# The last two channels of a convolution, score and batch-norm kernel: column sums by matmul, another order of the work, outputs from two engines

## The chip, the core and the metric

The kernel runs on one core of one Trainium2 chip. The metric is the device time of one execution in microseconds. Before the change it is 904.93 us, the median of three runs (902.93 to 905.02). The span of a profiled execution, from its first to its last instruction, is shorter than that execution's device time by what lies around it.

## The reference

Two layers, on x of shape 4 x 64 x 256 x 256 (batch, channel, row, column), float32. The first is a two-dimensional causal convolution per channel with a kernel that is an outer product of two length-256 filters, plus a bias term. The second takes, per image, the Gram matrix of the 256 rows, weighs it elementwise, sums it along its last axis, adds that one number per row to the row, and normalises each channel over the whole batch:

```python
def _L1_conv_ref(x, weights, gamma, beta):
    inv_dim = 1.0 / jnp.sqrt(jnp.asarray(D, dtype=x.dtype))
    scores = jnp.einsum('bpsd,bptd->bpst', x, x) * inv_dim
    red = jnp.sum(scores * weights[None], axis=-1, keepdims=True)
    y = x + red
    mean = jnp.mean(y, axis=(0, 2, 3), keepdims=True)
    var = jnp.var(y, axis=(0, 2, 3), keepdims=True)
    y_hat = (y - mean) * jax.lax.rsqrt(var + BN_EPS)
    return y_hat * gamma[None, :, None, None] + beta[None, :, None, None]
```

`red` below is that row sum. Nothing can be written of a channel before its mean and variance are known over all four images.

## The kernel before

The 64 channels go through a software pipeline, one channel per turn of the loop `for c in range(C + 4)` (line 360). Instructions are issued in the order of the program text on each engine (`manual_schedule`), so the text is the queue of every engine. A channel's x, 4 images of 256 x 256, is one buffer `x0` of 128 partitions x 2 pairs x 4 blocks x 256; a "pair" v holds two images, one in each half of the partitions.

Per channel c the stages are, with the turn in which they run:

- turn c-1: `conv_z` (line 173), the row convolution on PE, 64 matmul instructions on 64 x 64 quarters of the array; `copy_z` brings it out of PSUM on ACT.
- turn c: `conv_x0` (line 194), the column convolution on PE, 64 matmuls; four DVE operations (line 213) add the bias term and write `x0`. Then `gram` (line 226) for pair 0 and pair 1: 32 matmuls each, and after each `weigh` (line 251) for its two images and `spread` (line 266). `weigh` is three DVE operations for one image: two that multiply scores by weights and sum along the row into `red0` (line 257), and one that leaves products `pr`, whose sum over the partitions is still to be taken (line 261). `spread` puts `red0` on a diagonal (`eye_sb`) and adds it to `pr`, giving `sp`, two operations for one image (line 271).
- end of turn c: `all_sum` (line 276), one GpSimd sum over the partitions for all four images, 128 x 1024 (line 279), into `rd`.
- turn c+1: `pick_red` (ACT, line 286) brings the second image's half into place, `add_red` (line 288) adds `red` to `x0` with two DVE operations over 1024 elements that also sum it up (line 293), and GpSimd sums those sums over the partitions (line 297).
- turn c+2: `minus_mean` and two `squares` on ACT (lines 301 to 306), a GpSimd sum (312), `root` on ACT (318 to 322).
- turns c+3 and c+4: `scale_shift`, five small DVE operations (326 to 334), and four `finish` (line 339), each an ACT operation over 512 elements and an output transfer of 256 KB issued by SP (line 343). Output buffers: 4.

All tiles of PSUM come from one ring of eight banks. In the text of a turn, `conv_x0(c)` stands before `conv_z(c + 1)`, and the two `gram` of c stand last. So in turn 63 the column convolution of channel 63 follows both Gram matrices of channel 62 on PE, and its four DVE operations (line 213) follow `add_red(61)`, `weigh` and `spread` of channel 62 on DVE. After it PE has nothing but `gram(63, 0)` and `gram(63, 1)`. Turns 64 to 67 hold only the remaining statistics and outputs.

Of the kernel before, what the change touches and what calls it, by code (L numbers as in the profile page):

```python
# [8 lines left out]
F32 = mybir.dt.float32  # L9
AF = mybir.ActivationFunctionType  # L10
ALU = mybir.AluOpType
RED = bass_isa.ReduceOp
# [3 lines left out]
B, C, S = 4, 64, 256  # L16
P = 128
# [4 lines left out]
H = P // 2  # L22
BN_EPS = 1e-5
# [16 lines left out]
def conv_scores_bn_kernel(  # L40
# [70 lines left out]
    with tc.tile_pool(name="fps", bufs=2, space=PSUM) as fps:  # L111
        rhs = zT_sb
        for layer in range(3):
# [15 lines left out]
            rhs = h  # L129
# [63 lines left out]

    def conv_x0(c, z):


        xt = [xts.pop((c, v)) for v in range(2)]
        toep, x0 = hs.pop(c), st8[c][0]
        for m in range(2):
            p2 = [ps.tile([P, 2, S], F32, tag="ps", name=f"p2_{c}_{m}_{v}") for v in range(2)]  # L200
            for i in range(2):
                for k in range(4):
                    for t in range(4):
                        v, u = t % 2, t // 2
                        rows = bass.ts(v, H)
                        nc.tensor.matmul(  # L206
                            p2[v][bass.ts(u, H), i, : S - H * k],
                            lhsT=z[rows, u, k, bass.ts(2 * m + i, H)],
                            rhs=toep[rows, 0, H * k : S], start=(k == 0), stop=(k == 3),
                        )  # L210
            for v in range(2):
                part = bass.ts(m, 2)
                nc.vector.scalar_tensor_tensor(  # L213
                    x0[:, v, part], xt[v][:, part], chan_sb[:, 0, c : c + 1],
                    p2[v][:, :, ::-1], ALU.mult, ALU.add,
                )
# [9 lines left out]
    def gram(c, v):  # L226


        xb = st8[c][0].rearrange("p v i (t s) -> p v i t s", s=H)
        gs = [ps.tile([P, 8, H], F32, tag="ps", name=f"g_{c}_{v}_{u}") for u in range(2)]  # L230

        for places in (
            ((0, slice(0, 3), slice(0, 5, 2)), (1, slice(1, 4), slice(2, 7, 2))),
            ((2, slice(2, 4), slice(3, 7, 3)), (3, slice(0, 4, 3), slice(0, 4, 3))),
        ):
            for i in range(4):
                for n in range(4):
                    u, h = n % 2, n // 2
                    rows = bass.ts(u, H)
                    m, t, o = places[h]  # L240
                    nc.tensor.matmul(  # L241
                        gs[u][bass.ts(h, H), o, :],
                        lhsT=xb[rows, v, i, m, :], rhs=xb[rows, v, i, t, :],
                        start=(i == 0), stop=(i == 3),
                    )
# [20 lines left out]
    def spread(c, b):  # L266

        _, red0, sp, pr, _ = st8[c]
        for n in range(2):
            part = bass.ts(n, P)  # L270
            nc.vector.scalar_tensor_tensor(  # L271
                sp[:, b, part], eye_sb, red0[:, b, n : n + 1], pr[:, b, part],
                ALU.mult, ALU.add,
            )

    def all_sum(c):

        _, _, sp, _, rd = st8[c]
        nc.gpsimd.partition_all_reduce(  # L279
            rd.rearrange("p b s -> p (b s)"), sp.rearrange("p b s -> p (b s)"), P, RED.add  # L280
        )

    def pick_red(c):

        rd = st8[c][4].rearrange("p (v u) s -> p v u s", u=2)
        nc.scalar.copy(rd[H:, :, 0, :], rd[H:, :, 1, :])  # L286

    def add_red(c):
# [8 lines left out]
        nc.gpsimd.partition_all_reduce(mom[:, 2:4], mom[:, 0:2], P, RED.add)  # L297
        return mom

    def minus_mean(mom):  # L300
        nc.scalar.activation(mom[:, 4:5], mom[:, 2:3], AF.Identity, bias=mom[:, 3:4])  # L301
        nc.scalar.activation(mom[:, 5:6], mom[:, 4:5], AF.Identity, scale=-1.0 / (B * S * S))
# [33 lines left out]
        )  # L336
        return g, sh

    def finish(c, g, sh, v, n):
        part = bass.ts(n, 2)  # L340
        o = wk.tile([P, 2, S], F32, tag="o", name=f"o_{c}_{v}_{n}", bufs=4)
        nc.scalar.activation(o, st8[c][0][:, v, part], AF.Identity, bias=sh, scale=g)  # L342
        nc.sync.dma_start(out[c, v, n], o)

    for n in range(4):
        load_h(1, n)
# [5 lines left out]
    def begin_z(c):  # L352
        zs[c] = wk.tile([P, 2, 4, S], F32, tag="z", name=f"z_{c}")
# [3 lines left out]
        copy_z(0, u, conv_z(0, u))  # L357

    moms, scales, fins = {}, {}, {}
    for c in range(C + 4):  # L360
        p, q, f, e = c - 1, c - 2, c - 3, c - 4
        if c + 1 < C:
            copy_h(c + 1)
        if c < C:
            begin(c)
            conv_x0(c, zs.pop(c))

        if c + 1 < C:
            load_w(c + 1)
        if c + 2 < C:  # L370
            load_h(c + 2, 0)
        if 0 <= q < C:
# [8 lines left out]
        if 0 <= q < C:  # L381
            squares(q, moms[q], 1)
            tot = sum_squares(q, moms[q])
        if 0 <= f < C:
            fins[f] = (f, *scale_shift(f, moms.pop(f), *scales.pop(f)))
        if c + 1 < C:
            begin_z(c + 1)
            copy_z(c + 1, 0, conv_z(c + 1, 0))
# [6 lines left out]
        if c + 1 < C:  # L395
            copy_z(c + 1, 1, conv_z(c + 1, 1))
        if 0 <= f < C:
# [7 lines left out]
        if 0 <= q < C:  # L405
            scales[q] = root(q, tot)
        if 0 <= f < C:
            finish(*fins[f], 0, 1)
        if c + 3 < C:
            load_xt(c + 3, 1, 1)  # L410
        if c < C:
            gram(c, 0)
        if 0 <= p < C:
            moms[p] = add_red(p)
        if c < C:
            gram(c, 1)
            all_sum(c)


# [66 lines left out]
```

## Time and profile before

| What | Value |
|---|---|
| median of the runs | 904.93 us |
| the profiled execution, device time | 908.73 us |
| its span | 906.9 us |
| PE busy | 854.6 us (94%) |
| DVE busy | 757.4 us (84%) |
| ACT busy | 625.4 us (69%) |
| GpSimd busy | 442.8 us (49%) |
| last matmul of the kernel ends | 877.6 us |
| last ACT operation ends | 903.8 us |

Times within a trace are counted from the start of its span. A group's "mean ns of one" is the time from an instruction's start to its end; neighbours on DVE and ACT overlap by some tens of nanoseconds, so the step from one to the next is shorter (the line-293 operation has a mean of 1219 ns, and the step between two is 1150 ns). PE's records are two for each float32 matmul instruction. "PEclk" is the granted clock of PE as a share of full speed.

### The profile page before, as it was taken

Reading aid. Unit: us, or ns where it says so; the run is one execution under the profiler, and the core shown is the slowest. Engines: PE = TensorE matmul, PEld = TensorE weight load, DVE = VectorE, ACT = ScalarE, POOL = GpSimd, SP = SyncE. Lnnn points to the kernel's source line nnn. Section 1 sums busy time; section 2 is a strip of 40 time slices with the busy share of each in tenths; the row PEclk is TensorE's granted clock in tenths of the full one; section 3 lists DMA queues with packets and bytes.
Section 4 is the critical chain, followed back from the end, with each engine's and each line's share of the span. In section 5 each row is a group of like instructions: output and inputs, shape, how many; then the busy total and the mean of one; then the engine's idle time right before and its main releaser. Section 6 shows DMA issues by size and latency. Waiting matters only on the chain.

```text
span 906.9 us, 55787 instructions
## 1 busy us (share of the span) xinstructions
PE 854.6 (94%) x24584; PEld 824.9 (91%) x24584; DVE 757.4 (84%) x2648; ACT 625.4 (69%) x1220; POOL 442.8 (49%) x196
## 2 busy tenths in 40 slices
PE   2999999999999999999999999999999999999950
PEld 1999999999999999999999999999999988999950
DVE  3369888888988998898889889888988988988892
ACT  1237677677767767776777677677767767667756
POOL 0054455455455545644554554455455445445542
PEclk9999999999999999999999999999999999999985
DMA  5443665565556656565665656666665566556424
GB/s 157 133 136 126 202 206 194 182 205 194 200 199 208 198 194 211 198 195 198 207 195 194 213 186 198 199 207 198 201 205 194 191 194 198 189 192 206 133 74 160
DMA packets 89834, 169.42 MB, mean 187 GB/s; under 512 B 10614, under 2 KB 11832, under 8 KB 89592
## 3 DMA queue, kind: packets, MB, share of 16 engines
q1 hardware_dynamic: 88572, 164.95, 54.7%
q8 instruction: 193, 3.16, 1.5%
q10 hardware_dynamic: 1020, 0.90, 0.4%
q14 instruction: 49, 0.40, 0.2%
HBM read 97.91 MB, written 67.76 MB: 183 GB/s over the span
## 4 chain that ended last, share of the span: by engine, by line
PE 93%; DVE 3%; issue 1%; ACT 1%; POOL 1%; DMA 0%; ACTq 0%; DVEq 0%
PE p L183 31%; PE p L206 31%; PE g L241 31%; DVE x L293 1%; POOL rd L279 1%; ACT o L342 1%; DVE junk L257 0%; DVE sp L271 0%; PE ph L116 0%; DVE pr L261 0%; DVE fa L125 0%; DVE x L213 0%; DMA fw_sb<-in_fw 0%; DVE fa L118 0%; ACT sq L306 0%
## 5 line engine op out<-in xcount | busy, mean ns | idle before, releaser
L279 POOL PARTITION_ALL_REDUCE rd<-sp x64 | 391.9, 6123 | 198.5 <-DVE sp L271 196.0
L183 PE MATMUL p<-toep,xt 64*64 64x256 f32 (+3 forms) x8192 | 305.4, 298 | 5.8 <-issue 5.8
L206 PE MATMUL p<-toep,z 64*64 64x256 f32 (+3 forms) x8192 | 307.6, 297 | 2.7 <-issue 2.3
L241 PE MATMUL g<-x 64*64 64x192 f32 (+1 forms) x8192 | 305.4, 297 | 2.7 <-DVE x L213 2.5
L206 PEld LDWEIGHTS p<-toep,z 64*64 64x64 f32 x8192 | 291.9, 133 | 16.0 <-issue 5.6
L183 PEld LDWEIGHTS p<-toep,xt 64*64 64x64 f32 x8192 | 288.5, 134 | 16.5 <-issue 6.8
L241 PEld LDWEIGHTS g<-x 64*64 64x64 f32 x8192 | 289.5, 134 | 6.1 <-DVE x L213 3.0
L257 DVE SCALAR_TENSOR_TENSOR junk<-g,w 128x192 f32<-128x192 f32 x512 | 161.2, 352 | 93.2 <-PE g L241 93.2
L342 ACT ACTIVATE o<-x,sh,g 128x512 f32<-128x512 f32 x256 | 207.5, 813 | 2.0 <-DVE sh L334 2.0
L213 DVE SCALAR_TENSOR_TENSOR x<-xt,chan_sb,p 128x512 f32<-128x512 f32 x256 | 174.0, 743 | 9.6 <-PE p L206 9.6
L192 ACT COPY z<-p 128x512 f32<-128x512 f32 x256 | 135.3, 580 | 36.4 <-PE p L183 35.8
L293 DVE SCALAR_TENSOR_TENSOR x<-x,rd 128x1024 f32<-128x1024 f32 x128 | 151.3, 1219 | 5.7 <-ACT rd L286 5.7
L297 POOL PARTITION_ALL_REDUCE mom<-mom x64 | 25.6, 400 | 251.8 <-DVE x L293 244.1
L306 ACT ACTIVATE sq<-x,mom 128x1024 f32<-128x1024 f32 x128 | 146.5, 1145 | 2.3
L271 DVE SCALAR_TENSOR_TENSOR sp<-eye_sb,red,pr 128x128 f32<-128x128 f32 x512 | 144.7, 345 | 0.0
L261 DVE SCALAR_TENSOR_TENSOR pr<-g,w 128x256 f32<-128x256 f32 x256 | 107.4, 420 | 0.0
L286 ACT COPY rd<-rd 64x512 f32<-64x512 f32 x64 | 39.5, 617 | 92.3 <-POOL rd L279 92.3
L301 ACT ACTIVATE mom<-mom 128x1 f32<-128x1 f32 x64 | 19.0, 297 | 94.7 <-POOL mom L297 94.7
L151 ACT COPY toep<-toep 64x512 f32<-64x512 f32 x63 | 39.0, 619 | 32.2 <-DMA toep<-g_dram 19.3
L257 DVE DVE_READ_ACCUMULATOR junk<-g,w 128x1 f32 x512 | 42.8, 83 | 0.0
L312 POOL PARTITION_ALL_REDUCE tot<-mom x64 | 30.8, 481 | 3.8 <-ACT sq L306 3.8
L306 ACT ACTIVATION_READ_ACCUMULATOR sq<-x,mom 128x1 f32 x128 | 24.0, 188 | 0.0
(33 smaller groups left out, 171.1 us busy)
## 6 DMA issues: line engine op xcount, KB each, us to landing
xt<-in_xT SPq DMA_DIRECT2D x256, 256.0 KB
out<-o SPq DMA_DIRECT2D x256, 256.0 KB
w<-in_wl SPq DMA_DIRECT2D x64, 320.0 KB
toep<-g_dram SPq DMA_DIRECT2D x252, 36.0 KB
g_dram<-g_sb ACTq DMA_DIRECT2D x4, 80.0 KB
g_dram<-g_sb SPq DMA_DIRECT2D x4, 80.0 KB
fw_sb<-in_fw ACTq DMA_DIRECT2D x1, 192.0 KB
decay_sb<-in_decay ACTq DMA_DIRECT2D x1, 128.0 KB
```

Source lines behind the costliest of these rows:

```text
L183: nc.tensor.matmul(p1[u][bass.ts(v, H), k, : S - H * i], lhsT=xts[c, v][rows, i, bass.ts(2 * m + k, H)], rhs=toep[rows, 1, H * i : S], sta ...
L192: nc.scalar.copy(zs[c][:, u, bass.ts(m, 2), :], p1[u][:, :, ::-1])
L206: nc.tensor.matmul(p2[v][bass.ts(u, H), i, : S - H * k], lhsT=z[rows, u, k, bass.ts(2 * m + i, H)], rhs=toep[rows, 0, H * k : S], start=(k ...
L213: nc.vector.scalar_tensor_tensor(x0[:, v, part], xt[v][:, part], chan_sb[:, 0, c : c + 1], p2[v][:, :, ::-1], ALU.mult, ALU.add,)
L241: nc.tensor.matmul(gs[u][bass.ts(h, H), o, :], lhsT=xb[rows, v, i, m, :], rhs=xb[rows, v, i, t, :], start=(i == 0), stop=(i == 3),)
L257: nc.vector.scalar_tensor_tensor(junk, g[:, part, :], 1.0 / math.sqrt(S), w[:, 3 * n : 3 * n + 3, :], ALU.mult, ALU.mult, accum_out=red0[: ...
L261: nc.vector.scalar_tensor_tensor(pr[:, b].rearrange("p (t s) -> p t s", s=H), g[:, COL, :], 1.0 / math.sqrt(S), w[:, 6:10, :], ALU.mult, A ...
L271: nc.vector.scalar_tensor_tensor(sp[:, b, part], eye_sb, red0[:, b, n : n + 1], pr[:, b, part], ALU.mult, ALU.add,)
L279: nc.gpsimd.partition_all_reduce(rd.rearrange("p b s -> p (b s)"), sp.rearrange("p b s -> p (b s)"), P, RED.add)
L293: nc.vector.scalar_tensor_tensor(x0[:, v], x0[:, v], 1.0, rd[:, 2 * v, None, :].to_broadcast([P, 4, S]), ALU.mult, ALU.add, accum_out=mom[ ...
L306: nc.scalar.activation(sq, st8[c][0][:, v], AF.Square, bias=mom[:, 5:6], accum_out=mom[:, 6 + v : 7 + v])
L342: nc.scalar.activation(o, st8[c][0][:, v, part], AF.Identity, bias=sh, scale=g)
```

## The change

The loop runs over channels 0 to 62 only, and everything after it is written out in a new function `last_channels(63)`. Within the loop the instructions of turns 0 to 61 are the same. In turn 62 `gram(62, 1)`, its `weigh`, all `spread` of channel 62 and `all_sum(62)` are gone from the loop. `red` of channels 62 and 63 is taken by `red_by_pe`: for each half of the partitions three matmuls into PSUM, one with a matrix of ones over `pr` (256 columns) and two with `red0`, repeated over 64 columns, over the identity (128 columns each). `add_red_of` adds it from PSUM. In `last_channels` the column convolution of channel 63 stands in front of the second half of channel 62's Gram matrix. The squares of channel 63 are taken around the mean of its first pair, and corrected by five small DVE operations afterwards. The outputs of the last three channels are shared between DVE and ACT, and there are 8 output buffers instead of 4. The constant `ones` is set once at the start.

```diff
+    ones = const.tile([P, H], F32, name="ones")
+    nc.vector.memset(ones, 1.0)
...
+    def gram(c, v, weighed=True):
...
+        if not weighed:
+            banks.extend((g,) for g in gs)
+            return
         for u in range(2):
             weigh(c, 2 * v + u, gs[u])
-        for u in range(2):
-            spread(c, 2 * v + u)
+        if c < C - 2:
+            for u in range(2):
+                spread(c, 2 * v + u)
...
+    def red_by_pe(c, v):
+        _, red0, _, pr, _ = st8[c]
+        rp = ps.tile([P, S], F32, tag="ps", name=f"rp_{c}_{v}")
+        for u in range(2):
+            b, half = 2 * v + u, bass.ts(u, H)
+            nc.tensor.matmul(rp[half], lhsT=ones, rhs=pr[:, b], start=True, stop=False)
+            for n in range(2):
+                nc.tensor.matmul(
+                    rp[half, bass.ts(n, P)], lhsT=red0[:, b, n : n + 1].to_broadcast([P, H]),
+                    rhs=eye_sb, start=False, stop=(n == 1),
+                )
+        return rp
+
+    def add_red_of(c, v, rp, mom):
+        x0 = st8[c][0]
+        nc.vector.scalar_tensor_tensor(
+            x0[:, v], x0[:, v], 1.0, rp[:, None, :].to_broadcast([P, 4, S]),
+            ALU.mult, ALU.add, accum_out=mom[:, v : v + 1],
+        )
...
+    def finish(c, g, sh, v, n, vector=False):
         part = bass.ts(n, 2)
-        o = wk.tile([P, 2, S], F32, tag="o", name=f"o_{c}_{v}_{n}", bufs=4)
+        o = wk.tile([P, 2, S], F32, tag="o", name=f"o_{c}_{v}_{n}", bufs=8)
+        if vector:
+            nc.vector.tensor_scalar(o, y, g, sh, ALU.mult, ALU.add)
...
+    def last_channels(c):
+        p, q, f, e = c - 1, c - 2, c - 3, c - 4
+        begin(c)
+        finish(*fins[e], 1, 0)
+        finish(*fins[e], 1, 1)
+        conv_x0(c, zs.pop(c))
+        minus_mean(moms[q])
+        squares(q, moms[q], 0)
+        squares(q, moms[q], 1)
+        tot = sum_squares(q, moms[q])
+        fins[f] = (f, *scale_shift(f, moms[f], *scales[f]))
+        finish(*fins[f], 0, 0)
+        mom_p = sm.tile([P, 8], F32, tag="mom", name=f"mom_{p}")
+        add_red_of(p, 0, red_by_pe(p, 0), mom_p)
+        gram(p, 1)
+        scales[q] = root(q, tot)
+        finish(*fins[f], 0, 1)
+        gram(c, 0, weighed=False)
+        add_red_of(p, 1, red_by_pe(p, 1), mom_p)
+        nc.gpsimd.partition_all_reduce(mom_p[:, 2:4], mom_p[:, 0:2], P, RED.add)
+        finish(*fins[f], 1, 0)
+        finish(*fins[f], 1, 1)
+        for u in range(2):
+            weigh(c, u, *banks.pop(0))
+        minus_mean(mom_p)
+        squares(p, mom_p, 0)
+        squares(p, mom_p, 1)
+        tot_p = sum_squares(p, mom_p)
+        gram(c, 1)
+        mom = sm.tile([P, 8], F32, tag="mom", name=f"mom_{c}")
+        add_red_of(c, 0, red_by_pe(c, 0), mom)
+        nc.gpsimd.partition_all_reduce(mom[:, 2:3], mom[:, 0:1], P, RED.add)
+        rp = red_by_pe(c, 1)
+        add_red_of(c, 1, rp, mom)
+        fins[q] = (q, *scale_shift(q, moms[q], *scales[q]))
+        half = 2.0 / (B * S * S)
+        nc.scalar.activation(mom[:, 5:6], mom[:, 2:3], AF.Identity, scale=-half)
+        squares(c, mom, 0)
+        scales[p] = root(p, tot_p)
+        squares(c, mom, 1)
...
+        nc.gpsimd.partition_all_reduce(sums[:, 1:2], mom[:, 1:2], P, RED.add)
+        nc.gpsimd.partition_all_reduce(sums[:, 2:4], mom[:, 6:8], P, RED.add)
+        for v in range(2):
+            for n in range(2):
+                finish(*fins[q], v, n, vector=n == 0)
+        fins[p] = (p, *scale_shift(p, mom_p, *scales[p]))
+        d = sums[:, 4:5]
+        nc.vector.tensor_scalar(d, sums[:, 1:2], mom[:, 2:3], half / 2, ALU.subtract, ALU.mult)
+        nc.vector.tensor_scalar(mom[:, 5:6], mom[:, 5:6], d, None, ALU.subtract)
+        nc.vector.tensor_scalar(sums[:, 5:6], d, d, -BN_EPS, ALU.mult, ALU.add)
+        nc.vector.tensor_scalar(
+            sums[:, 6:7], sums[:, 2:3], sums[:, 3:4], half / 2, ALU.add, ALU.mult
+        )
+        v = sums[:, 7:8]
+        nc.vector.tensor_scalar(v, sums[:, 6:7], sums[:, 5:6], None, ALU.subtract)
+        r = sm.tile([P, 1], F32, tag="r", name=f"r_{c}")
+        nc.scalar.activation(r, v, AF.Sqrt)
+        for i in range(2):
+            finish(*fins[p], i, 0)
+            finish(*fins[p], i, 1, vector=True)
+        fins[c] = (c, *scale_shift(c, mom, v, r))
+        for i in range(2):
+            finish(*fins[c], i, 0)
+            finish(*fins[c], i, 1, vector=True)
...
-    for c in range(C + 4):
+    for c in range(C - 1):
...
         gram(c, 0)
-        if 0 <= p < C:
+        if p >= 0:
             moms[p] = add_red(p)
-        if c < C:
+        if c < C - 2:
             gram(c, 1)
             all_sum(c)
+    last_channels(C - 1)
```

More of the change, by code (lines that the diff above doesn't have):

```diff
@@ L224, in begin @@
         st8[c] = (x0, red0, sp, pr, rd)
-    def gram(c, v):
+    banks = []
+    def gram(c, v, weighed=True):
         xb = st8[c][0].rearrange("p v i (t s) -> p v i t s", s=H)
@@ L337, in scale_shift @@
         return g, sh
-    def finish(c, g, sh, v, n):
+    def finish(c, g, sh, v, n, vector=False):
         part = bass.ts(n, 2)
-        o = wk.tile([P, 2, S], F32, tag="o", name=f"o_{c}_{v}_{n}", bufs=4)
-        nc.scalar.activation(o, st8[c][0][:, v, part], AF.Identity, bias=sh, scale=g)
-        nc.sync.dma_start(out[c, v, n], o)
+        o = wk.tile([P, 2, S], F32, tag="o", name=f"o_{c}_{v}_{n}", bufs=8)
+        y = st8[c][0][:, v, part]
+        if vector:
+            nc.vector.tensor_scalar(o, y, g, sh, ALU.mult, ALU.add)
+        else:
+            nc.scalar.activation(o, y, AF.Identity, bias=sh, scale=g)
+        nc.sync.dma_start(out[c, v, n], o)
@@ new lines, in last_channels @@
+    def last_channels(c):
[38 more added lines that the diff above has]
+        squares(c, mom, 1)
+        tot = sm.tile([P, 3], F32, tag="tot", name=f"tot_{c}")
+        sums = sm.tile([P, 8], F32, tag="sums", name=f"sums_{c}", bufs=1)
+        nc.gpsimd.partition_all_reduce(sums[:, 1:2], mom[:, 1:2], P, RED.add)
[22 more added lines that the diff above has]
+            finish(*fins[c], i, 1, vector=True)
@@ L359, in conv_scores_bn_kernel @@
     moms, scales, fins = {}, {}, {}
-    for c in range(C + 4):
+    for c in range(C - 1):
         p, q, f, e = c - 1, c - 2, c - 3, c - 4
-        if c + 1 < C:
-            copy_h(c + 1)
-        if c < C:
[L365 to L369, printed above, removed]
+        begin(c)
+        copy_h(c + 1)
+        conv_x0(c, zs.pop(c))
+        load_w(c + 1)
         if c + 2 < C:
             load_h(c + 2, 0)
-        if 0 <= q < C:
+        if q >= 0:
             minus_mean(moms[q])
@@ L380, in conv_scores_bn_kernel @@
             load_xt(c + 3, 0, 0)
-        if 0 <= q < C:
+        if q >= 0:
             squares(q, moms[q], 1)
             tot = sum_squares(q, moms[q])
-        if 0 <= f < C:
+        if f >= 0:
             fins[f] = (f, *scale_shift(f, moms.pop(f), *scales.pop(f)))
-        if c + 1 < C:
-            begin_z(c + 1)
-            copy_z(c + 1, 0, conv_z(c + 1, 0))
+        begin_z(c + 1)
+        copy_z(c + 1, 0, conv_z(c + 1, 0))
         if e >= 0:
@@ L394, in conv_scores_bn_kernel @@
             load_xt(c + 3, 1, 0)
-        if c + 1 < C:
-            copy_z(c + 1, 1, conv_z(c + 1, 1))
-        if 0 <= f < C:
+        copy_z(c + 1, 1, conv_z(c + 1, 1))
+        if f >= 0:
             finish(*fins[f], 0, 0)
@@ L402, in conv_scores_bn_kernel @@
             load_xt(c + 3, 0, 1)
-        if 0 <= p < C:
+        if p >= 0:
             pick_red(p)
-        if 0 <= q < C:
+        if q >= 0:
             scales[q] = root(q, tot)
-        if 0 <= f < C:
+        if f >= 0:
             finish(*fins[f], 0, 1)
@@ L410, in conv_scores_bn_kernel @@
             load_xt(c + 3, 1, 1)
-        if c < C:
-            gram(c, 0)
-        if 0 <= p < C:
+        gram(c, 0)
+        if p >= 0:
             moms[p] = add_red(p)
-        if c < C:
+        if c < C - 2:
             gram(c, 1)
             all_sum(c)
+    last_channels(C - 1)
 def kernel(**inputs):
```

## The prediction

> **What bounds the kernel now.** The page comes first: its span, the shares of the chain that ended last, and the slices. For 877 of 906.9 us the chain is PE's matmuls, and the change leaves PE's instructions of that stretch as they are. So the gain is to be sought in the end, where PE has stopped.
>
> ```profile
> span 906.9 us, 55787 instructions
> PE   2999999999999999999999999999999999999950
> PE 93%; DVE 3%; issue 1%; ACT 1%; POOL 1%; DMA 0%; ACTq 0%; DVEq 0%
> ```
>
> Second, the chain of waits in order of time (start, us, what). After channel 63's last `spread` DVE stops, GpSimd sums for 6.13 us, ACT copies, DVE adds: all in a row.
>
> ```profile
> 881.93 1.05 DVE sp L271 x4
> 882.98 0.08 DVE r L326
> 883.06 0.08 issue
> 883.14 6.13 POOL rd L279
> 889.28 0.02 issue
> 889.30 0.63 ACT rd L286
> 889.92 0.02 issue
> 889.95 2.38 DVE x L293 x4
> ```
>
> Third, the timeline of the end: the Gram matrices of channel 63 wait for its column convolution, and the last seven outputs come from ACT alone, one each 0.74 us.
>
> ```profile
> 869.88 2.71 DVE L213 SCALAR_TENSOR_TENSOR x<-xt,chan_sb,p 128x512 f32<-128x512 f32 x4
> 870.67 0.88 PE L241 MATMUL g<-x 64*64 64x192 f32 x16 [2.07 <-DVE x L213]
> 871.99 5.60 PE L241 MATMUL g<-x 64*64 64x192 f32 x112 [0.44 <-DVE x L213]
> 898.60 5.20 ACT L342 ACTIVATE o<-x,sh,g 128x512 f32<-128x512 f32 x7
> ```
>
> Fourth, stretches of it (us; busy PE, PE loads, DVE, ACT, GpSimd; clock, DMA share, GB/s). PE's clock falls to half after its idle time, and a burst of outputs fills the DMA engines at about 370 GB/s. No byte moves after 905.5, so 1.5 us of the span follow the last byte.
>
> ```profile
> 873.00:874.00 1.00, 1.00 (x24) 1.00 (x20) 0.74 (x4) 0.12 (x1) 1.00 (x1) 0.50 0.68 246
> 886.00:886.50 0.50, 0.00 (x0) 0.00 (x0) 0.00 (x0) 0.00 (x0) 0.50 (x1) 0.50 0.99 373
> 904.00:904.50 0.50, 0.00 (x0) 0.00 (x0) 0.00 (x0) 0.00 (x0) 0.00 (x0) 0.50 1.02 381
> 905.50:906.00 0.50, 0.00 (x0) 0.00 (x0) 0.00 (x0) 0.00 (x0) 0.00 (x0) 0.50 0.00 0
> ```
>
> **What the Trainium skill says.** "TensorE: Matmul & The Clock Gate", Part 1: PE runs at half clock after an idle window of about 3.4 us. The trace agrees in kind (0.50 after PE's gaps from 868.6 on). "VectorE: DVE Perf Modes", Mode 2×_2P: a float32 operation with a single tensor source and both sides in SBUF takes two elements per cycle; here TENSOR_SCALAR over 256 takes 294 ns (lines 122, 123) and SCALAR_TENSOR_TENSOR over 256 takes 425 ns (line 125). "DMA: Bandwidth & Descriptors", Specifications: 358 GB/s of HBM for a core, 368 in a cost model; the trace shows 373 and 381 in half microseconds. "TensorEngine Tiling (Array Packing)", Key Properties: a change of the tiling mode drains PE; `red_by_pe` (128 rows x 64 columns) among 64 x 64 tiles makes such changes, and no row of before shows their cost.
>
> **The change, part by part**, on the clock of the profiled execution.
>
> *Start and loop: nothing.* `ones` is a memset of 128 x 64 (0.11 us for such a one, line 101) while DVE has been idle up to 3.96 us. Eight output buffers take away waits of ACT on transfers that cost nothing: line 342's idle time is 2.0 us in all, behind DVE.
>
> *DVE from 863.85.* `pick_red(61)` ends at 863.83. Before, `spread` of channel 62 held DVE until 864.76; now `add_red(61)` starts at once: 2 x 1.15 = 2.29, to 866.14. Then come the four line-213 operations of channel 63, 2.71, to 868.85; their matmuls are ready, since `gram(62,0)` ends near 861.9 (half of 859.6 to 864.0), and `conv_x0(63)` takes 4.55, to 866.45. So channel 63's x is complete 3.7 us earlier than before (872.59). `scale_shift(60)`: 1.35 (872.51 to 873.84 before), to 870.2.
>
> *`red_by_pe`, unknown.* 128 records of `conv_z` with 2,560 column steps take 4.55 us, 1.78 ns per column. A half has 256+128+128 = 512 columns: 0.91 us if its loads (133 ns, two per matmul) are hidden; with all six in the open 0.91 + 0.80 = 1.7. Two halves use different columns of the array and might overlap, which gives a lower bound of 0.45 per half. I take 1.0, as loads of 133 ns exceed the 114 ns of a 128-column record, and 0.17 us from last issue to result (a 64-column record lasts 217 ns, of which 57 are columns).
>
> *PE*: `red_by_pe(62,0)` 866.45 to 868.45; `gram(62,1)` and `gram(63,0)`, 2.3 each (half of 4.6), to 873.05; `red_by_pe(62,1)` to 875.05, result 875.2; `gram(63,1)` to 877.35. PE has no gap until 877, so I keep full clock.
>
> *DVE on.* `add_red_of` reads PSUM: between 1.15 (line 293's step) and 1.36 (two line-213 steps of 0.68, 512 elements from PSUM); I take 1.25. Channel 62 pair 0 to 871.45; `weigh` of two images, 1.78 (861.93 to 863.71), to 873.23; then DVE waits 2.0 for `red_by_pe(62,1)`. Pair 1 to 876.45. `weigh` of channel 63, 4 x 0.89, to 880.0. Pair 0 of 63 to 881.25. Its last sums: image 1 is weighed at 878.23, three halves on PE follow, to 881.25 + 0.17 = 881.4; pair 1 to 882.65. Before this was 892.33. **Gain so far 9.7 us**: the GpSimd sum with its copy (883.14 to 889.92) and the 3.7 us of the order, less the new waits on PE.
>
> *Statistics.* The sum of pair 0 starts 0.16 after 881.25, takes 0.40 (line 297), ACT's mean 0.2; squares from 882.1: 1.25 (893.49 to 894.74), `root(62)` 0.7, squares 1.25, to 885.3, GpSimd to 885.8. DVE meanwhile: `scale_shift(61)` to 884.0; two outputs, estimated 294 + 133 = 0.43 each, to 884.85; `scale_shift(62)` to 886.2; five small operations of 0.26, to 887.5. So here DVE, not the squares, ends last, and squaring from the first pair's mean gains nothing by itself. Square root to 887.8, two outputs of 62 on DVE to 888.35, `scale_shift(63)` to 889.7. From complete x to known scale: 7.05 us, before 7.54 (892.33 to 899.87).
>
> *Outputs.* ACT makes two of channel 62 from 887.8 (0.74 each), two of 63 by 891.2; DVE's are ready sooner. SP issues in program order, 0.35 apart: the first of 62 at 888.6, the last of 63 at 891.6. From an issue (883.29) to its bytes is 0.75 us; 256 KB at 370 GB/s is 0.71; after the last byte 1.5. Eight outputs in a burst: 888.6 + 0.75 + 8 x 0.71 + 1.5 = 896.5. Production alone would give 891.6 + 0.75 + 0.71 + 1.5 = 894.6. **The transfers take back 1.9 us of what sharing the outputs gives.** From known scale to the end stays near 7 us (before 899.87 to 906.9).
>
> *Sum.* 906.9 - 896.5 = 10.4 us, of which 9.7 from `red` and order, 0.5 from the statistics, 0.2 from the outputs. The profiled execution would go from 908.73 to 898.3; it lies 3.8 above the median, so the gain comes off the median: 904.93 - 10.4 = 894.5 us.
>
> **The rivals.** *Outputs do not queue:* DMA engines show 0.99 to 1.02 of their time busy in such a burst, which speaks against it, but channel 62 could be out sooner. Then 894.6 ends the span: 892.6 us. *`red_by_pe` is slow, or PE cools:* loads in the open (0.7 more for each of seven halves in series: 4.9), or half clock in the waits after 875 (two to three halves and half of a Gram matrix, about 4): 898 to 899.5. For it: the mode changes and loads into the same rows; against it: PE is fed without a gap until 877. *Slower than before:* both together. Each `red_by_pe` drains PE, loads in the open and runs at half clock, 3.4 us for a half; seven in series are 7 x 2.4 = 17 us more, 911 us. It decides from 1.0 + (10.4 + 2.7)/7 = 2.9 us for a half. The trace shows half clock only after gaps of PE, and nothing that lengthens loads threefold. *The change doesn't do what it says*, a wait on a PSUM bank that holds the column convolution back: the ring of eight gives it banks freed at 860.9 and 863.7, so I see none; with it `red` alone would still be worth 6 us: 899.
>
> **How the numbers follow.** Forecast 894.5 with chance 0.55 (893 to 896.5 of its own); outputs don't queue 0.15; slow or cool PE, or the bank, 0.25; slower 0.03; what is left, 0.02, near no change. The range reaches from 891.5 (the second case with `red_by_pe` at 0.45) to 898.8. A measurement of this kernel tells 0.3% (2.7 us) from no change. Faster 0.95, same 0.02, slower 0.03.
>
> **What would show it.** No GpSimd sum of 6 us after 863.2; `add_red_of` of channel 63's second pair ending near 882.6; a half of `red_by_pe` near 1.0 us; DVE idle about 2 us before `add_red_of` of channel 62's pair 1; DVE's small operations, not the squares, ahead of the square root; the DMA engines full from 889.4 to 895. I am wrong if the loop's turns change length, if a half takes 2 us or more, or if the last bytes follow the last issue with no queue.

## The result, and the profile after

The change makes the kernel faster: 893.89 us (median of 6 runs, 890.46 to 895.64) against 905.34 us (6 runs, 902.93 to 907.40) for the kernel before on the same chip. The ratio is 0.9865, with a 95% interval of 0.9838 to 0.9892, a gain of 11.45 us (9.8 to 14.7 by that interval). The prediction had 894.5 and 10.4.

The profiled execution of after took 891.24 us, and its span of 889.2 is 17.7 shorter than that of before. Not all of this is the change's. But for one small memset and the number of output buffers, both kernels contain the same instructions up to channel 61's GpSimd sum (128 x 1024). It starts at 857.04 before and at 851.04 after, so 6.0 us of the difference arose in the loop before it. Some turns of the loop last longer than the usual 13.08 us, and each execution has its own number of them. All comparisons of traces below therefore use one number, **T: from the start of channel 61's GpSimd sum to the end of the span**. Before it is 906.9 - 857.04 = 49.86 us, after 889.2 - 851.04 = 38.16 us, so the end gained 11.7 us. "rel" below counts from that start. In the trace of before it is this line (the same line of after stands below):

```profile
857.04 6.13 POOL L279 PARTITION_ALL_REDUCE rd<-sp  x1 [2.43 <-DVE sp L271]
```

The page of after (span; busy share of PE and granted PE clock in 40 slices; shares of the chain that ended last):

```profile
span 889.2 us, 55809 instructions
PE   2999999999999999999999999999999999999993
PEclk9999999999999999999999999999999999999997
PE 96%; DVE 2%; issue 1%; ACT 0%; DMA 0%; ACTq 0%; DVEq 0%
```

GpSimd has left the chain altogether (1% before), and PE's part rose from 93% to 96%: PE is now busy into the last slice instead of leaving that one and half of the one before empty.

The chain of waits of after in order of time (start, us, what):

```profile
872.36 0.51 PE rp L314 x2
872.87 0.44 PE rp L316 x4
873.31 0.39 PE rp L314 x2
873.70 0.45 PE rp L316 x4
874.15 0.02 issue
874.17 1.23 DVE x L324 x2
...
881.72 0.28 DVE sh L363
882.01 0.03 issue
882.03 0.81 ACT o L375
882.85 0.71 ACTq L581
```

PE carries the chain until 874.15 (rel 23.1); the two halves of `red_by_pe(63,1)` are 0.51 + 0.44 = 0.95 and 0.39 + 0.45 = 0.84 us in it. Channel 63's x is complete at 875.40 (rel 24.4; before 892.33, rel 35.3). The last scale is known at 882.0.

The timeline of after (start, duration, engine, line, operation; in brackets the idle time before it and who ended it):

```profile
851.04 6.12 POOL L287 PARTITION_ALL_REDUCE rd<-sp  x1 [2.43 <-DVE sp L279]
868.21 1.22 DVE L324 SCALAR_TENSOR_TENSOR x<-x,rp 128x1024 f32<-128x1024 f32 x1 [1.17 <-PE rp L316]
876.70 1.00 DVE L373 TENSOR_SCALAR o<-x,g,sh 128x512 f32<-128x512 f32 x2
877.87 1.50 ACT L375 ACTIVATE o<-x,sh,g 128x512 f32<-128x512 f32 x2
```

851.04 is the last 128 x 1024 sum of the kernel; those of channels 62 and 63 are gone. DVE's wait for PE (the second line) is 1.17 us. Two outputs take DVE 1.00 and ACT 1.50. Note the third and fourth line: DVE has two outputs of channel 61 ready by 877.7, but ACT makes its first only from 877.87, since `squares` of channel 63 stands in front.

Stretches of after (from:to and length, us; busy PE, PE loads, DVE, ACT, GpSimd; PE clock, DMA share, GB/s):

```profile
872.00:874.00 2.00, 2.00 (x16) 1.47 (x14) 2.00 (x7) 1.12 (x2) 0.40 (x1) 1.00 0.00 0
879.00:879.50 0.50, 0.00 (x0) 0.00 (x0) 0.39 (x4) 0.37 (x1) 0.00 (x0) 0.83 0.00 0
879.50:880.00 0.50, 0.00 (x0) 0.00 (x0) 0.47 (x4) 0.07 (x1) 0.00 (x0) 0.50 0.94 348
885.00:886.00 1.00, 0.00 (x0) 0.00 (x0) 0.00 (x0) 0.00 (x0) 0.00 (x0) 0.50 1.02 377
887.00:887.50 0.50, 0.00 (x0) 0.00 (x0) 0.00 (x0) 0.00 (x0) 0.00 (x0) 0.50 0.42 156
887.50:888.00 0.50, 0.00 (x0) 0.00 (x0) 0.00 (x0) 0.00 (x0) 0.00 (x0) 0.50 0.00 0
```

PE runs at full clock while it still has work; its clock drops around 879, when it has none. The last burst of transfers starts at 879.5, fills the DMA engines, and ends at about 887.2. In these 7.7 us eleven outputs of 256 KB go out, 0.70 us each. Some 2.0 us of the span follow the last byte.

### The profile page after: what moved, and what is told of

Same layout as the page of the kernel before. It is cut to its first block, busy times and chain, and to the rows that moved or that the text cites. A ratio compares the mean times of both kernels' runs of the same rounds, so it can differ in the third digit from the quotient of the medians.

```text
span 889.2 us, 55809 instructions
## 1 busy us (share of the span) xinstructions
PE 855.8 (96%) x24632; PEld 818.4 (92%) x24632; DVE 757.5 (85%) x2644; ACT 615.8 (69%) x1209; POOL 430.9 (48%) x195
## 4 chain that ended last, share of the span: by engine, by line
PE 96%; DVE 2%; issue 1%; ACT 0%; DMA 0%; ACTq 0%; DVEq 0%
PE p L185 32%; PE p L208 32%; PE g L245 31%; PE ph L118 0%; PE rp L314 0%; PE rp L316 0%; DVE fa L127 0%; DMA fw_sb<-in_fw 0%; DVE fa L120 0%; DVE o L373 0%; ACT fh L130 0%; PE ph_out L133 0%; DVE x L324 0%; DVE fk L125 0%; DVE fa L128 0%
## 5 line engine op out<-in xcount | busy, mean ns | idle before, releaser
L287 POOL PARTITION_ALL_REDUCE rd<-sp x62 | 379.6, 6122 | 193.8 <-DVE sp L279 193.8
L185 PE MATMUL p<-toep,xt 64*64 64x64 f32 (+3 forms) x8192 | 304.3, 298 | 5.8 <-issue 5.8
L208 PE MATMUL p<-toep,z 64*64 64x64 f32 (+3 forms) x8192 | 303.4, 297 | 0.7 <-issue 0.5
L185 PEld LDWEIGHTS p<-toep,xt 64*64 64x64 f32 x8192 | 283.9, 134 | 20.8 <-issue 6.8
L245 PE MATMUL g<-x 64*64 64x192 f32 (+1 forms) x8192 | 300.9, 296 | 0.0
L208 PEld LDWEIGHTS p<-toep,z 64*64 64x64 f32 x8192 | 285.2, 134 | 16.7 <-issue 1.3
L245 PEld LDWEIGHTS g<-x 64*64 64x64 f32 x8192 | 286.4, 134 | 2.3 <-issue 0.3
L375 ACT ACTIVATE o<-x,sh,g 128x512 f32<-128x512 f32 x250 | 201.6, 809 | 0.7 <-DVE sh L363 0.7
L301 DVE SCALAR_TENSOR_TENSOR x<-x,rd 128x1024 f32<-128x1024 f32 x124 | 146.6, 1219 | 0.1
L279 DVE SCALAR_TENSOR_TENSOR sp<-eye_sb,red,pr 128x128 f32<-128x128 f32 x496 | 140.2, 344 | 0.0
L294 ACT COPY rd<-rd 64x512 f32<-64x512 f32 x62 | 38.2, 616 | 93.0 <-POOL rd L287 92.9
L335 ACT ACTIVATION_READ_ACCUMULATOR sq<-x,mom 128x1 f32 x128 | 23.9, 186 | 0.0
```

The source lines that it names most:

```text
L185: nc.tensor.matmul(p1[u][bass.ts(v, H), k, : S - H * i], lhsT=xts[c, v][rows, i, bass.ts(2 * m + k, H)], rhs=toep[rows, 1, H * i : S], sta ...
L208: nc.tensor.matmul(p2[v][bass.ts(u, H), i, : S - H * k], lhsT=z[rows, u, k, bass.ts(2 * m + i, H)], rhs=toep[rows, 0, H * k : S], start=(k ...
L245: nc.tensor.matmul(gs[u][bass.ts(h, H), o, :], lhsT=xb[rows, v, i, m, :], rhs=xb[rows, v, i, t, :], start=(i == 0), stop=(i == 3),)
L279: nc.vector.scalar_tensor_tensor(sp[:, b, part], eye_sb, red0[:, b, n : n + 1], pr[:, b, part], ALU.mult, ALU.add,)
L287: nc.gpsimd.partition_all_reduce(rd.rearrange("p b s -> p (b s)"), sp.rearrange("p b s -> p (b s)"), P, RED.add)
L301: nc.vector.scalar_tensor_tensor(x0[:, v], x0[:, v], 1.0, rd[:, 2 * v, None, :].to_broadcast([P, 4, S]), ALU.mult, ALU.add, accum_out=mom[ ...
```

## The experiments

T below comes from the trace of one execution of each kernel. Where a device time is given too, it is a median of several runs, and its ratio is to the kernel before on the same chip. The controls come first, because a single trace is only worth something if T repeats.

| Run | What differs | T, us | against after (38.14) |
|---|---|---|---|
| c_before | the kernel before | 50.05 | +11.9 |
| c_after, c2_after | after, on two chips | 38.14, 38.12 | 0 |
| e1_act_outs | all outputs on ACT | 39.02 | +0.9 |
| e2_full_mean | squares from the mean of both pairs | 39.16 | +1.0 |
| e6_old_order | column convolution behind Gram | 37.97 | -0.2 |
| e9_sum_alone | e1, e2 and e6 together: the sum by PE is what is left | 40.37 | +2.2 |
| e5_pool_sum | sums back on GpSimd | 53.26 | +15.1 |
| e3_half_bytes | half the bytes of the last outputs | 36.52 | -1.6 |
| e7_bufs8 | before, with 8 output buffers | 48.89 | +10.8 |
| e4_early61 | channel 61's outputs earlier | 37.25 | -0.9 |
| e8_early_both | those of 61 and 62 earlier | 35.45 | -2.7 |

**Controls.**

> The kernel before once more, as a control of T. Theory 1 (T of before depends only on whether PE's clock drops to half in channel 63's Gram matrices): T is 49.9 us with clock 0.5 there, as in the first trace, or 48.9 with clock 1.00, as with eight output buffers. Theory 2: T lies elsewhere by 0.7 us or more, and the gain of T is not known to better than that.

> The changed kernel once more, as a control. T is the time from the start of channel 61's GpSimd sum (128 x 1024) to the end of the span: 49.9 us in the trace of before (906.9 - 857.0), 38.2 in that of after (889.2 - 851.0). Theory 1: what differs between executions of one kernel lies in the loop's turns, so T comes out within 0.5 us of 38.2 whatever the span is. Theory 2: the end varies too, then T lies 1 us or more away and single traces of the experiments can't be compared by T.

> The changed kernel on the same chip as the one before, for comparison with it. Both theories: T 38.2 within 0.3; ratio to before 0.984 to 0.990.

T is 49.86 and 50.05 for before, 38.16, 38.14 and 38.12 for after. In after, c_after, c2_after, e1 and e2, whose work on PE and DVE is the same up to there, channel 63's x is complete at rel 24.35 each time. The start of channel 61's sum meanwhile lies at 851.04, 863.56 and 855.68 in the three executions of after, and on one single chip at 863.56 to 869.53 in seven executions of after and its variants. So one trace tells differences in T above some 0.2 us, and the span doesn't tell 5 us. Six runs of c2_after had a median of 897.02 (895.46 to 901.74), ratio 0.9866 (0.9823 to 0.9910), the first result again.

**e1_act_outs: are the shared outputs worth something?**

```diff
-        if vector:
+        if False:
```

> All twelve outputs of channels 61 to 63 by ACT, none by DVE. Theory 1 (the outputs are bound by their transfers, 0.69 us each, in either kernel): ACT makes one in 0.74 us, so it is only a little slower than the transfers: the last output is issued near 2.7 us later than in after, with no queue behind it, and T rises by 0.5 to 1.2 us, to 38.7 to 39.4. Theory 2 (two engines at the outputs are a main part of the gain): six outputs back on ACT are 4.4 us more in its queue, T rises by 3 us or more, to 41 or above.

T grew by 0.9, within the 0.5 to 1.2 of the first theory. Two stretches of e1 and, below them, two of after:

```profile
896.00:896.50 0.50, 0.00 (x0) 0.00 (x0) 0.00 (x0) 0.50 (x2) 0.00 (x0) 0.50 0.08 29
904.00:905.00 1.00, 0.00 (x0) 0.00 (x0) 0.00 (x0) 0.00 (x0) 0.00 (x0) 0.50 1.00 373
```

```profile
878.00:878.50 0.50, 0.00 (x0) 0.00 (x0) 0.43 (x3) 0.50 (x1) 0.41 (x1) 1.00 0.76 287
878.50:879.00 0.50, 0.00 (x0) 0.00 (x0) 0.46 (x3) 0.50 (x2) 0.00 (x0) 1.00 0.64 238
```

In e1 the burst begins at 896.45 (rel 28.5, as in after) and is full until 905.0: 8.6 us, the time of twelve outputs. In after, 287 and 238 GB/s over half a microsecond each are 262 KB: one output, the first that DVE made, is gone before the burst begins, and eleven remain. ACT alone makes one output in 0.72 us (eight in 5.73), about the 0.70 in which the queue takes one, so the faster making in the middle of the burst brings little: what sharing gives is that one output ahead of it.

**e2_full_mean: is squaring from the first pair's mean worth something?**

```diff
-        nc.gpsimd.partition_all_reduce(mom[:, 2:3], mom[:, 0:1], P, RED.add)
...
+        nc.gpsimd.partition_all_reduce(mom[:, 2:4], mom[:, 0:2], P, RED.add)
...
-        squares(c, mom, 0)
         scales[p] = root(p, tot_p)
+        minus_mean(mom)
+        squares(c, mom, 0)
         squares(c, mom, 1)
...
+        tot = sum_squares(c, mom)
...
+        v, r = root(c, tot)
```

> The squares of channel 63 wait for the mean of both pairs, without the five correcting operations on DVE; channel 62's root moves in front of them. Theory 1 (DVE's small operations and the transfers end last, not the squares): T within 0.7 us of 38.2, since the squares start 1.7 us later but 0.9 us of corrections go and the transfers are full either way. Theory 2 (squaring from the first pair's mean is worth its 1.15 us plus the wait for the second sum): T rises by 1.5 us or more.

T grew by 1.0. Its timeline and two stretches of it:

```profile
890.40 1.00 DVE L373 TENSOR_SCALAR o<-x,g,sh 128x512 f32<-128x512 f32 x2
...
891.54 1.15 ACT L335 ACTIVATE sq<-x,mom 128x1024 f32<-128x1024 f32 x1
...
892.68 1.50 ACT L375 ACTIVATE o<-x,sh,g 128x512 f32<-128x512 f32 x2
```

```profile
893.00:894.00 1.00, 0.00 (x0) 0.00 (x0) 0.70 (x2) 1.00 (x2) 0.74 (x1) 0.50 0.00 0
894.00:895.00 1.00, 0.00 (x0) 0.00 (x0) 0.16 (x1) 0.97 (x5) 0.00 (x0) 0.50 0.67 250
```

T fits neither theory; it lies between them. The scale of channel 63 is known only 0.4 later than in after (from T's start: 31.3 against 31.0). But the later `squares` also hold back the outputs of channel 61 that ACT makes: the first starts at 892.68 (rel 27.9; after 877.87, rel 26.8). SP issues in program order, so the outputs that DVE has ready wait behind it, and the burst begins at about 894.35 (rel 29.6; after rel 28.5). A queue that is full from end to end passes on its start: 1.1 later at its head, 1.0 at its end.

**e6_old_order: is the new order worth something?** `gram(p, 1)` goes back in front of the column convolution.

```diff
+        gram(p, 1)
         conv_x0(c, zs.pop(c))
...
-        gram(p, 1)
```

> The column convolution of channel 63 stands again behind the whole Gram matrix of channel 62; the sums by PE, statistics and outputs are those of after. Theory 1 (DVE bounds this stretch, its work is the same in either order, and the 1.17 us it waits for PE take up the rest): T within 0.5 us of 38.2. Theory 2 (the order itself is worth the 2 to 3.7 us that the prediction gave to it): T 40 to 42.

T fell by 0.2: beside the sum by PE, the new order is worth nothing. Three pieces of its chain of waits:

```profile
876.50 4.58 PE p L208 x92
...
891.94 0.45 PE rp L316 x4
...
892.42 1.23 DVE x L324 x2
```

Here too PE works through to `red_by_pe` of the last pair, and x is complete at 893.65, rel 24.1 (after 24.4), so the new order rather costs 0.2 us. In either order PE then holds the chain from the convolution to the last sums, with the same work (the two pairs of `red_by_pe(62)` take 1.50 us each here, 1.50 and 1.87 in after). What the order would be worth without the sum by PE was not measured.

**e9_sum_alone: e1, e2 and e6 in one kernel.** What is left of the change is the sum by PE (and what goes with it: no `spread`, no GpSimd sum, no copy, for two channels), the 8 buffers, and the text of `last_channels`, which makes the outputs of channel 61 later than before does.

> Only the sum over the partitions of channels 62 and 63 by PE: the column convolution in the old order, the squares from the full mean, all twelve outputs of channels 61 to 63 by ACT. Theory 1 (the sum by PE, with spread and the copy gone, is nearly the whole gain; the rest is worth 0.9 and 1.0 us as measured singly): T 39.5 to 40.5. Theory 2 (the parts need one another, as the slow run with GpSimd in the new order might suggest): T 43 or above.

T is 40.37, 9.5 below before and within the first theory's range. Its chain shows how the gain comes and how part of it goes back:

```profile
882.03 1.23 DVE x L324 x2
...
886.94 2.82 ACT o L375 x4
```

x of channel 63 is complete at 883.26, rel 23.9, which is 11.4 earlier than before (35.3). But from there to the end it takes 16.4 us instead of 14.6 before. In e9 ACT makes all four outputs of channel 61 (886.94) between complete x and the last scale, and all eight of channels 62 and 63 after them. In before it makes three outputs in that place (894.64 and 896.49):

```profile
890.66 0.80 ACT L342 ACTIVATE o<-x,sh,g 128x512 f32<-128x512 f32 x1
...
894.64 0.80 ACT L342 ACTIVATE o<-x,sh,g 128x512 f32<-128x512 f32 x1
...
896.49 1.51 ACT L342 ACTIVATE o<-x,sh,g 128x512 f32<-128x512 f32 x2
```

Of the four outputs in these lines the first, at 890.66, comes before x is complete (892.33); it is channel 61's second, and its first was made beside the GpSimd sum. The shared outputs and the first pair's mean win these 1.9 us back, and more: after needs 13.8 us from complete x to the end. Taken out singly they cost 0.9 and 1.0, together with the order 2.2, so about 0.5 comes only where both are there.

**e5_pool_sum: the other way round, everything but the sum by PE.**

```diff
-        add_red_of(p, 0, red_by_pe(p, 0), mom_p)
         gram(p, 1)
+        all_sum(p)
...
-        gram(c, 0, weighed=False)
-        add_red_of(p, 1, red_by_pe(p, 1), mom_p)
+        gram(c, 0)
+        gram(c, 1)
+        all_sum(c)
...
+        pick_red(p)
+        add_red_by_pool(p, mom_p)
```

> The sum over the partitions of channels 62 and 63 goes back to GpSimd (with spread on DVE and the copy on ACT), in the new order of the convolution, with the new statistics and the shared outputs. T as before, from the start of channel 61's GpSimd sum to the end. Theory 1 (taking the sum from GpSimd and spread from DVE is nearly the whole gain of 11.7 us): the two sums of 6.13 us run back to back, channel 63's x is complete about 8 us later than in after, T 45.5 to 47. Theory 2 (the order and the outputs carry the gain): T 40 to 42.

53.26 fits neither theory: it is longer than the T of before. The timeline says why:

```profile
884.01 6.12 POOL L286 PARTITION_ALL_REDUCE rd<-sp  x1 [2.71 <-DVE sp L278]
885.54 3.94 DVE L278 SCALAR_TENSOR_TENSOR sp<-eye_sb,red,pr 128x128 f32<-128x128 f32 x4
...
892.48 6.95 POOL L286 PARTITION_ALL_REDUCE rd<-sp  x1 [2.34 <-DVE sp L278]
893.37 5.55 DVE L310 SCALAR_TENSOR_TENSOR x<-x,rd 128x1024 f32<-128x1024 f32 x1
```

Four `spread` operations, 1.12 us when GpSimd is idle, took 3.94 beside its sum; the second `add_red` operation of channel 62 took 5.55, and the sum beside it 6.95 instead of 6.12. Both kinds read two tensors from SBUF. The 2.8 and 4.3 us are together about what T lies above the 45.5 to 47 of the first theory. The first `add_red` operation (at 892.23) took its usual 1.21, though the sum began 0.25 us after it and ran beside the rest, so not every part of a sum slows such an operation. The `weigh` operations beside the first of these sums, with one operand in PSUM, kept their 0.34 to 0.36 for `junk` and 0.42 for `pr`. The Trainium skill states it in "GPSIMD Engine Reference", 1. Specifications: GpSimd's SBUF interfaces are shared with VectorE, with contention for DVE instructions that have two SBUF inputs; "SBUF — State Buffer", Who interferes with whom, says it of a GpSimd instruction that reads SBUF. This run agrees and gives the price. In before neither kind runs beside such a sum (in one turn, `spread` ends at 842.78, the sum lasts from 842.95 to 849.07, the next `spread` starts at 850.63). So e5 measures the collision together with the sum, and doesn't give the sum's own worth. For that there is e9.

**e7_bufs8: do the 8 buffers do something by themselves?** The kernel before, with `bufs=8` for the outputs.

```diff
-        o = wk.tile([P, 2, S], F32, tag="o", name=f"o_{c}_{v}_{n}", bufs=4)
+        o = wk.tile([P, 2, S], F32, tag="o", name=f"o_{c}_{v}_{n}", bufs=8)
```

> The kernel before with eight output buffers instead of four, nothing else changed. Theory 1 (the buffers do nothing; the 6 us by which the loop was shorter in the one trace of after is scatter between executions): the ratio to before lies within 0.4% of 1, and T within 0.3 us of 49.9. Theory 2 (fewer waits of ACT on transfers shorten the loop): the ratio is 0.996 or lower.

The device time is 915.33 us (20 runs), ratio 1.0009 (0.9986 to 1.0031), no difference. Yet its T is 48.89, 1.0 to 1.2 below the two traces of before and outside the first theory's 0.3. A stretch within `gram(63)`, first of c_before, then of e7:

```profile
880.00:881.00 1.00, 1.00 (x20) 0.85 (x16) 0.81 (x4) 0.00 (x0) 1.00 (x1) 0.50 0.76 262
```

```profile
879.00:880.00 1.00, 1.00 (x36) 0.96 (x36) 0.86 (x4) 0.00 (x0) 1.00 (x1) 1.00 0.31 98
```

c_before did 20 matmul records there in a microsecond at clock 0.50, e7 36 at 1.00. Its x of channel 63 is complete at rel 34.5 instead of 35.3 in the trace of before: 0.8 of the difference is in this stretch, the rest, 0.15, behind the last scale. So in both executions of before PE was at half clock there, and in the one of e7 it was not. PE's idle time just before `gram(63)` doesn't tell them apart: 2.07 and 2.08 us where the clock fell, 2.14 where it didn't, all shorter than the 3.4 us of idle time that the prediction gives as the condition. Whether the buffers have to do with it, or the chip (e7 and c_before were on different ones), stays open. Against a before with full clock the sum by PE alone gives 48.9 - 40.4 = 8.5.

**e3_half_bytes: do the last transfers queue?** The last twelve outputs are written by half only.

```diff
+        if c < C - 3:
+            nc.sync.dma_start(out[c, v, n], o)
+        else:
+            nc.sync.dma_start(out[c, v, n][:, 0:1], o[:, 0:1])
```

> The transfers of the last three channels carry the first half of each output buffer only; all computation stays. Theory 1 (the end waits for a queue of transfers that began with channel 61): the last transfer follows its issue without a queue, the end comes 1.5 to 2.5 us sooner, T 35.7 to 36.7. Theory 2 (the end is bound by making and issuing the outputs): T within 0.4 us of 38.2.

T fell by 1.6, as the first theory had it. Two stretches of it:

```profile
898.00:899.00 1.00, 0.00 (x0) 0.00 (x0) 0.00 (x0) 0.00 (x0) 0.00 (x0) 0.50 0.80 266
899.00:900.00 1.00, 0.00 (x0) 0.00 (x0) 0.00 (x0) 0.00 (x0) 0.00 (x0) 0.50 0.04 12
```

With half the bytes the engines move 266 GB/s at a share of 0.80, no longer full, and 128 KB take 0.49 us. So the bytes of the last outputs account for 1.6 us of T, the shorter transfer of the very last one included. What sets the 0.49 was not separated.

**e4_early61 and e8_early_both: can the burst begin earlier?** e4 takes `scale_shift(61)` and its outputs in front of channel 63's statistics. e8 does this for channel 62's as well, except for one output of each, and swaps the engines that make channel 63's:

```diff
+        rp_p = red_by_pe(p, 1)
+        fins[q] = (q, *scale_shift(q, moms[q], *scales[q]))
+        add_red_of(p, 1, rp_p, mom_p)
...
+        finish(*fins[q], 0, 0)
+        finish(*fins[q], 0, 1)
...
+        finish(*fins[q], 1, 0)
+        scales[p] = root(p, tot_p)
...
+        fins[p] = (p, *scale_shift(p, mom_p, *scales[p]))
...
+        finish(*fins[p], 0, 0, vector=True)
+        finish(*fins[q], 1, 1, vector=True)
+        finish(*fins[p], 1, 0)
+        finish(*fins[p], 1, 1)
...
+        finish(*fins[p], 0, 1, vector=True)
```

> Channel 61's scale is worked out while DVE waits for the second sum by PE of channel 62, and its four outputs are made by ACT in its idle time around 868 to 870 and 873 to 875, so that eight instead of twelve outputs stand in the last burst and DVE has 2.3 us less between channel 63's x and its scale. Theory 1 (the burst of transfers that begins with channel 61 sets the end): it begins with channel 62 instead, and the last output lands 2 to 3 us sooner: T 35.2 to 36.2, median about 891.5 against about 894 of after. Theory 2 (the statistics of channel 63 set the end, transfers don't queue): only DVE's 0.9 us come off, T about 37.3.

> Beyond the early channel 61: channel 62's root goes in front of the squares of channel 63, its scale follows channel 63's x at once, and its outputs start before the five correcting operations, so that the burst of transfers begins about 2 us sooner than with channel 61 early alone (T 37.3). Theory 1 (the time from the first output of the last eight to the end is that of eight transfers plus 2.7 us): T 35 to 36, median 2 to 3 us below that of after on the same chip. Theory 2 (the scale of channel 63 now ends last): T about 36.5.

T is 37.25 for e4 (-0.9) and 35.45 for e8 (-2.7). e4 has the T of its second theory but not its reason: the transfers do queue. Its burst begins with channel 62, as in the first theory, but at 897.25 (rel 29.7), 1.2 later than that of after; that takes back 1.2 of the 2.1 us of the three outputs that it has less. A stretch of e4:

```profile
901.00:902.00 1.00, 0.00 (x0) 0.00 (x0) 0.00 (x0) 0.00 (x0) 0.00 (x0) 0.50 1.04 389
```

Two stretches of e8:

```profile
890.00:890.50 0.50, 0.00 (x0) 0.00 (x0) 0.47 (x3) 0.50 (x2) 0.00 (x0) 1.00 1.04 385
895.00:896.00 1.00, 0.00 (x0) 0.00 (x0) 0.00 (x0) 0.00 (x0) 0.00 (x0) 0.50 0.99 377
```

The DMA engines are full at rel 27.3 and still at rel 33, but the last byte leaves some 2.7 earlier than in after. The device time doesn't show it: six runs of e8 had 899.05 (894.87 to 903.21), ratio 0.9874 (0.9833 to 0.9915), and c2_after on the same chip 897.02 with 0.9866 (0.9823 to 0.9910). e4, on another chip, had 903.55, ratio 0.9871 (0.9831 to 0.9910). The loop's scatter of several us covers a gain of 2.7 in six runs, so whether e8 beats after remains open; that its end is shorter is what the trace of one execution shows.

## Why the prediction was right, point by point

The forecast held: 894.5 against 893.89. Its sum for the end was 10.4, and T gained 11.7. The working is right in its large part and wrong in how it divides the gain. That the forecast lies within 0.6 us of the result is in part luck. The gain up to complete x was put 1.25 too low and that of the statistics 0.45 too low, and from the last scale to the end the 6.8 of the working stands near the measured 7.2 although the burst of outputs was another one. And with six runs instead of three the median of before came out 0.4 higher.

- **Start and loop: nothing.** Right. The 8 buffers give a ratio of 1.0009 (e7), and the loop's 6.0 us between the two profiles is of the size by which executions on one chip differ (controls).
- **"Gain so far 9.7 us": complete x at rel 25.6.** It came at rel 24.4, so 10.9. The column convolution's x was written at rel 11.8, as predicted. The difference is the wait "DVE waits 2.0 for `red_by_pe(62,1)`", which was 1.17, and `add_red_of`, whose step is 1.14 and not 1.25. The wait is shorter mostly because the two halves of `red_by_pe(62,0)` together took 1.50 us, where the working has 2.0, because the convolution's matmuls ended 0.2 sooner, and because the latency of 0.17 is hardly there: DVE starts 0.02 to 0.04 after the modelled end of the last record.
- **A half of `red_by_pe`, taken as 1.0 within 0.45 to 1.7.** 0.83 to 0.84 for the second half of a pair; 0.95 to 1.06 for the first where it stands apart, and 1.50 for both of `red_by_pe(62,0)`, whose records interleave. The rival "slow, or PE cools" is gone: clock 1.00 up to about 879, and for the drain at a change of tiling mode, which the prediction took from the Trainium skill ("TensorEngine Tiling (Array Packing)", Key Properties), the trace leaves no more than the 0.17 to 0.26 us for which PE's weight loads stand idle at such changes; whether that is the drain is not shown.
- **"The 3.7 us of the order".** This step failed, though the sum didn't. e6 puts the order back and loses nothing. What makes the stretch shorter is, by the durations, what the sum by PE removes: `spread`, 8 operations of 0.26 or 2.1 us for each channel on DVE, and GpSimd's 6.13 us with ACT's copy at the very end, 11.0 us in all, near e9's 11.4 (10.6 against e7, at full clock); no run takes them apart. The prediction booked the missing `spread` of channel 62 under "order", because it saw DVE come sooner to the convolution's x and took this for the effect of the move. The rest of the 3.7 is `weigh` of channel 62's second pair (1.78), which the new order only puts off.
- **"The squaring from the first pair's mean gains nothing by itself."** Wrong, 1.0 us (e2). The prediction looked only at who ends last ahead of the square root. There it was right, DVE's small operations do (the five take 0.93, to 879.89), and the squares cost just 0.4 at the scale. It missed the queue: the same `squares` stands in front of channel 61's outputs on ACT, and the first of these starts the burst.
- **Outputs: "a burst of eight from 888.6", DMA full from rel 32.4; sharing gives 0.2.** It was eleven, from rel 28.5, starting with channel 61's second; sharing gives 0.9, since one output is out ahead of the burst (e1). An output on DVE, estimated at 0.43, took 0.50. The end at rel 38.2 and not 39.5 has three parts: complete x 1.25 earlier; from there to the last scale 6.6 and not 7.05; and from the scale to the end 7.2 and not 6.8, since the last byte is followed by 2.0 us and not 1.5.
- **"The transfers take back 1.9 us."** Right in kind and near in size: halving the bytes gives 1.6 (e3), with transfers that still follow one another at 0.49 us. The rival "outputs do not queue" is refuted by the full DMA engines.
- **A part of the gain that the working doesn't name:** some 0.8 us of the 11.7 goes with the half clock in `gram(63)` of before, since x was complete that much sooner in the one execution at full clock (e7). What decides the clock there is open. The trace of before gave the prediction its end with the half clock in it, so its total holds this part.

By worth: the sum by PE 9.5 (e9; 8.5 against a before at full clock), shared outputs 0.9 (e1), the first pair's mean 1.0 (e2), the order nothing (-0.2, e6), and about 0.5 that the parts give only together, in all 11.7. Each of these is a difference between single traces.

## What to carry to other kernels

Where the end of a pipeline hangs on a cross-partition sum on a slow engine, a few matmuls with ones or an identity into PSUM can do it in less time and piece by piece (here 1.5 to 1.9 us for a pair of images, against 6.1 for all four at once), and they remove the preparation on other engines as well; count that preparation with the sum, not with the reordering that comes along. If the last stretch is a full output queue, its end is its beginning plus the bytes: look for what delays the **first** outputs, also on an engine that isn't the one that ends last, and on a queue that issues in order. To compare ends of long kernels, measure from an instruction that both share; the span of a single execution can move by more than the change.

## What the runs showed of the hardware

- A DVE operation with two tensors in SBUF beside a 128 x 1024 GpSimd sum took 5.55 us instead of 1.21, and the sum 6.95 instead of 6.12 (e5); one that began 0.25 us before the sum was not slowed (1.21). DVE operations with one operand in PSUM were not touched (0.34 to 0.36).
- The same code went through one stretch at PE clock 0.50 in two executions of before and at 1.00 in the one of e7 (5.60 and 5.23 against 3.93 us for the same 112 records of `gram(63)`), with an effect of 0.8 us on complete x. PE's idle time before it was 2.07, 2.08 and 2.14 us.
- After the last byte 1.9 to 2.0 us pass until the span ends in after and its variants (e9 included), but 1.5 to 1.6 in before, c_before and e7. So the prediction read its 1.5 rightly; why the new end takes 0.4 us longer is open.
- The start of channel 61's sum, after the same instructions, varied from 851.04 to 869.53 us over the executions profiled.
